# A planner's durations set to the trace, and a tile's scores ordered behind the values of the tile ahead

## The chip, the core and the metric

The kernel runs on one core of a Trainium2 chip. The metric is the device time of one execution in microseconds (us), as the median of several runs. In the profile PE is TensorE (matmuls), PEld its weight loads, DVE is VectorE, ACT is ScalarE, POOL is GpSimd and SP is the engine whose queue issues nearly all transfers.

## What is computed

The input x is 8 sequences of 512 tokens with 256 channels, all in float32. The program is a sandwich of three blocks:

```
x = x + 0.5 * ffn(layernorm(x))      # "local" block, two layers
x = x + attn(layernorm(x))           # global attention, 16 heads of 16 channels
x = x + 0.5 * ffn(layernorm(x))      # the local block again, same weights

ffn, for each of 2 layers:
  h = shift_token(x)                 # second half of the channels one token later
  q, k, v = split(h @ wqkv)          # 8 heads of 64
  q, k = rotary(l2norm(q) * qs), rotary(l2norm(k) * ksc)
  x = x + local_attention(q, k, v) @ wo     # windows of 128: own and previous window
  h = layernorm(shift_token(x)) * lg + lb
  a, g = split(h @ w1 + b1)
  x = x + (a * gelu(g)) @ w2 + b2
attn, for each of 16 heads:
  softmax(y y^T / 4) x, then times a 256x256 slice of the weight, summed over heads
```

## The kernel before

Three streams of work run side by side. Streams 0 and 1 each take eight local blocks, for the even and the odd sequences (`stream`, `attention`, `glu`). The third, `global`, does the global attention of a sequence as soon as its first local block is done (`global_heads`), and fills the holes of the other two. A sequence's 512 tokens are four tiles of 128. In `attention` a tile goes through `front` (projections, norms, rotary), `scores` (matmuls of q and k, mask and maximum, exp, division), `values` (probabilities times v) and `project`. Scores and values come in two groups of four heads, `g` = 0 and 1; each group has one buffer of probabilities, `work_p`, of which a stream has two.

The first and the last local block of a stream turn the probabilities on TensorE. All others are "far" (`far` is true): they are turned by VectorE in 32x32 pieces and by a round trip through DRAM. There `turned_quarters` writes a buffer with two transfers to `dram_quarters` and reads it back with four; `turned_far` does the same for smaller ones with one write. Both run on SP's queue.

Nothing is issued when it is written down. The code records operations in a `Plan`; every call becomes an `Op`, and consecutive matmuls inside `plan.together()` become one. `Plan.order` is then a list scheduler over five engines. It gives each operation a time that the engine is busy and a time until its result is there (`Plan.cost`), knows which operations each one must follow (`op.after`, found from the tiles that they read and write), and picks again and again the operation that can start earliest by its model; among those that can start within 40 ns of it, the one recorded first (`rank`). It also decides which slot of a buffer or PSUM bank a tile gets. `Plan.issue` emits the instructions in that order, so the planner's durations decide the order in which each engine's queue stands, and nothing else. All five engines run their queues in order and wait on semaphores. As every instruction is emitted from `issue`, all carry one line number in the profile, and groups are told apart by tile names.

The planner knows that TensorE's array works in several shapes (`op.mode`: whole, 64x64 "quarters", 32-row "fours") and charges 150 ns (290 into "fours") for a change of shape (`Plan.MODE`); a matmul in another shape than the last one gets a rank 100 lower in priority (`Plan.STICK`). A change of ScalarE's function table is charged 1283 ns (`Plan.TABLE`). Transfers go through one modelled pipe (`pipe`):

```
            if op.calls[0][0] == "dma_start":
                a = op.calls[0][2]["out"]
                pipe = max(pipe, op.start + 2000.0) + elements(a) * a.shape[0] * 4 / 170
                op.end = pipe + 300
```

The number at the end is bytes per ns. The functions that the change touches:

Of the kernel before, what the change touches and what calls it, by code (L numbers as in the profile page):

```python
# [13 lines left out]
PSUM, DRAM = bass.MemoryType.PSUM, bass.MemoryType.DRAM  # L14

P = 128
# [153 lines left out]
def elements(a):  # L170
    n = 1
    for d in a.shape[1:]:
        n *= d
    return n


class Plan:
# [55 lines left out]
    def cost(self, op):  # L233

        if op.engine == "tensor":

            lanes, op.mode = {}, "whole"
            for name, args, kw in op.calls:
                lane, t = 0, 109.0
                if name == "matmul":  # L240
                    a = kw["lhsT"]
                    lane, t = (a.region()[0], args[0].region()[0]), 2 * max(0.842 * elements(kw["rhs"]), 0.852 * a.shape[1])
                    k, m = a.shape
                    op.mode = "fours" if k <= 32 else "quarters" if k <= 64 and m <= 64 else "halves" if k <= 64 else "columns" if m <= 64 else "whole"
                lanes[lane] = lanes.get(lane, 0.0) + t
            busy = max(lanes.values())
            return busy, busy + 170
        name, args, kw = op.calls[0]
        n = max(elements(a) for a in (*args, *kw.values()) if hasattr(a, "shape"))
        if name == "dma_start":  # L250
            return 580.0, 2300.0
        if op.engine == "scalar":
            if name == "activation":
                op.mode = {AF.Exp: "exp", AF.Gelu: "gelu"}.get(args[2])
                busy = 70 + 0.82 * n + (105 if "bias" in kw else 0)
                return (busy + 93, busy + 310) if "accum_out" in kw else (busy, busy + 110)
            return 70 + 0.81 * n, 175 + 0.81 * n
        if op.engine == "vector":
            if name == "tensor_tensor_reduce":
                return 90.0 + n, 250.0 + n  # L260
            if name == "bn_stats":
                return 70.0 + n, 150.0 + n
            return 90 + 1.035 * n, 170 + 1.035 * n
        if name == "memset":
            return 80 + 0.85 * n, 100 + 0.85 * n
        if ALU.pow in args:
            return 350.0 + 157 * n, 400.0 + 157 * n
        return 210 + 1.98 * n, 250 + 1.98 * n

    def order(self):  # L270

        for op in self.ops:
            op.busy, op.done = self.cost(op)
            op.waits = len(op.after)
            for o in op.after:
                o.before.append(op)

            for t in op.tiles:
                if t.users[0] is op:
                    source = [] if t.ring.space == PSUM else [u for u in op.tiles if u.ring.space == PSUM and u.users[0] is not op]  # L280
                    (source[0].users[0] if source else op).opens.append(t)
        for op in self.ops:
            op.opens.sort(key=lambda t: t.turn)
            for t in op.opens:
                for o in t.users:
                    if o is not op:
                        op.admits.append(o)
                        o.waits += 1
        free, mode = dict.fromkeys(self.ENGINES, 0.0), dict.fromkeys(self.ENGINES)
        pipe = 0.0  # L290
        candidates = {e: [op for op in self.ops if op.engine == e and not op.waits] for e in self.ENGINES}
        order = []

        def slots(op):

            need, turns, at = {}, {}, 0.0
            for t in op.opens:
                k, i = need.get(t.ring, 0), turns.get((t.ring, t.stream), 0)
                need[t.ring], turns[t.ring, t.stream] = k + 1, i + 1
                if t.ring.space != PSUM:  # L300

                    k += t.ring.missing(t.stream, t.turn) - i
                if len(t.ring.free) <= k:
                    return None
                at = max(at, t.ring.free[k][0])
            return at

        while len(order) < len(self.ops):
            best = None
            for e in self.ENGINES:  # L310
                when = []
                hold = min((op.rank for op in candidates[e] if len(op.opens) > 4 and op.ready <= free[e]), default=None)
                for op in candidates[e]:
                    if op.opens:
                        at = slots(op)
                        if at is None:
                            continue
                        if hold is not None and op.rank > hold and op.opens[0].ring.space == PSUM:
                            continue
                        at = max(at, op.ready, free[e])  # L320
                    else:
                        at = max(op.ready, free[e])
                    when.append((at, op))
                if when:
                    t = min(at for at, _ in when)
                    if best is None or t < best[0]:
                        best = t, e, when
            assert best is not None, "the plan is stuck"
            t, e, when = best
            change = self.MODE.get(mode[e], 0.0) if e == "tensor" else self.TABLE if e == "scalar" else 0.0  # L330
            switch = lambda op: change if op.mode is not None and op.mode != mode[e] else 0.0
            at, op = min(
                ((at, op) for at, op in when if at <= t + 40), key=lambda c: (c[1].rank + (self.STICK[e] if switch(c[1]) else 0), c[0])
            )
            candidates[e].remove(op)
            op.start = at + switch(op)
            mode[e] = op.mode or mode[e]
            free[e] = op.start + op.busy
            op.end = op.start + op.done
            if op.calls[0][0] == "dma_start":  # L340
                a = op.calls[0][2]["out"]
                pipe = max(pipe, op.start + 2000.0) + elements(a) * a.shape[0] * 4 / 170
                op.end = pipe + 300
            for x in op.opens:
                _, x.slot = x.ring.free.pop(0)
                x.ring.open(x.stream, x.turn)
            for x in op.tiles:
                x.left -= 1
                x.end = max(x.end, op.end)
                if not x.left:  # L350
                    x.ring.free.append((x.end + self.SIGNAL, x.slot))
                    x.ring.free.sort()
            for o in op.before:
                if o.engine != e:
                    o.ready = max(o.ready, op.end + self.SIGNAL)
                elif e != "tensor":
                    o.ready = max(o.ready, op.end)
            for o in op.before + op.admits:
                o.waits -= 1
                if not o.waits:  # L360
                    candidates[o.engine].append(o)
            order.append(op)
        return order
# [12 lines left out]
def macaron(ctx: ExitStack, tc: tile.TileContext, x, weight, wqkv, wo, w1, w2, b2, vecs, qk_scales, rotary, out):  # L376
# [87 lines left out]
    for i, sign in enumerate((1, -1, 1)):  # L464
# [5 lines left out]
            base=0,  # L470
# [95 lines left out]
    def attention(k, y, l, far):  # L566
# [2 lines left out]
        tiled = lambda t, c: y[:, t, c * P : (c + 1) * P]  # L569
        nc.scalar.copy(z0[:, :N], transposed(tiled, 0))  # L570
        z1 = shifted(tiled, k)
        v = {}

        kT = work.tile([P, NPAIR, 2, P], F32, tag=f"kT{k}", bufs=1)

# [54 lines left out]
        def scores(t, pair, rn):  # L630
# [21 lines left out]
            for g in range(2):  # L652
# [16 lines left out]
                with plan.together():  # L669
                    for i in range(2):  # L670
                        keys = kT[:, 2 * g + i].rearrange("p j k -> p (j k)")
                        for q, to, ks in sorted(pieces, key=lambda piece: piece[1].start - piece[1].stop):
                            for par in range(2):
                                rows = slice(par * DH, (par + 1) * DH)
                                nc.tensor.matmul(
                                    sps[par][q, i, to], lhsT=qT[rows, 2 * g + i, q], rhs=keys[rows, ks], start=True, stop=True
                                )
                heads = slice(4 * g, 4 * g + 4)

                if far:  # L680
# [51 lines left out]
        def values(t, probs):  # L732
# [25 lines left out]
            if far:  # L758
                for g in range(2):
                    with plan.together():  # L760
                        for i in range(2):
                            products(
                                2 * g + i,
                                lambda par, own, rows, q: probs[g][rows, own * (nk - 1), q.start // 32 : q.stop // 32, 2 * i + par, :],
                            )
            else:
                turned = []
                for n in range(NPAIR + 2):
# [370 lines left out]
```

## Time and profile before

| | us |
|---|---|
| median of 3 runs | 3949.23 (3947.79 to 3949.27) |
| the profiled execution's own time | 3952.0 |
| its span, first to last instruction | 3950.1 |
| PE busy (matmuls) | 3878.5 |
| VectorE, ScalarE, GpSimd busy | 2447.9, 1766.9, 1233.7 |

The span holds 26240 records of matmuls, since each float32 matmul stands as two, and some are missing. A row of groups reads: line, engine, operation, tile written and tiles read, shape, count; then busy time, mean ns of one, and the engine's idle time just before with what ended it. A row of waits reads: engine and tile that waited, who released it, us in total, times, longest. A row of windows reads: the stretch and its length, busy us and instructions of each engine, then the granted clock of TensorE, the share of the transfer engines and GB/s. Matmuls overlap in their records, so that one's record is longer than the time until the next one starts.

### The profile page before, as it was taken

Reading aid. Unit: us, or ns where it says so; the run is one execution under the profiler, and the core shown is the slowest. Engines: PE = TensorE matmul, PEld = TensorE weight load, DVE = VectorE, ACT = ScalarE, POOL = GpSimd, SP = SyncE. Lnnn points to the kernel's source line nnn. Section 1 sums busy time; section 2 is a strip of 40 time slices with the busy share of each in tenths; the row PEclk is TensorE's granted clock in tenths of the full one; section 3 lists DMA queues with packets and bytes.
Section 4 is the critical chain, followed back from the end, with each engine's and each line's share of the span. In section 5 each row is a group of like instructions: output and inputs, shape, how many; then the busy total and the mean of one; then the engine's idle time right before and its main releaser. Section 6 shows DMA issues by size and latency. Waiting matters only on the chain.

```text
span 3950.1 us, 72878 instructions
## 1 busy us (share of the span) xinstructions
PE 3878.5 (98%) x26240; PEld 2659.5 (67%) x26240; DVE 2447.9 (62%) x6888; ACT 1766.9 (45%) x4548; POOL 1233.7 (31%) x1132
## 2 busy tenths in 40 slices
PE   8999999999999999999999999999999999999998
PEld 4566776766767667677676776767767667686665
DVE  7676655667566665674765747657466565535674
ACT  5565534535344353452443534535335353324564
POOL 6242323424133341341422405324133242103240
PEclk9999999999999999999999999999999999999999
DMA  3000543534435344253442534525335244110000
GB/s 116 1 24 27 155 135 104 150 98 140 129 104 153 93 128 143 88 165 92 128 138 94 155 104 130 159 91 156 91 116 157 81 143 134 61 33 9 1 24 11
DMA packets 437644, 400.74 MB, mean 101 GB/s; under 512 B 53954, under 2 KB 379172, under 8 KB 437284
## 3 DMA queue, kind: packets, MB, share of 16 engines
q1 hardware_dynamic: 436420, 394.76, 33.5%
q8 instruction: 208, 3.41, 0.4%
q10 hardware_dynamic: 864, 1.33, 0.1%
q14 instruction: 152, 1.25, 0.1%
HBM read 235.49 MB, written 143.66 MB: 96 GB/s over the span
## 4 chain that ended last, share of the span: by engine, by line
PE 81%; DVE 5%; issue 2%; ACT 2%; POOL 1%; DMA 0%; SPq 0%; DVEq 0%; POOLq 0%; ACTq 0%
PE psum_bank L369 81%; ACT work_p L369 2%; DVE work_p L369 2%; DVE work_qn L369 1%; DVE small_ss L369 1%; POOL small_rn L369 0%; POOL work_t L369 0%; ACT work_both L369 0%; DVE work_xw L369 0%; DVE small_bnst L369 0%; SPq L369 0%; DVE work_both L369 0%; DVE work_o L369 0%; DVE xpool_x L369 0%; POOL small_rstd L369 0%
## 5 line engine op out<-in xcount | busy, mean ns | idle before, releaser
L369 PE MATMUL psum_bank<-work_xw,work_e 128*128 128x256 f32 x4096 | 960.0, 385 | 3.0 <-ACT work_e L369 1.9
L369 PEld LDWEIGHTS psum_bank<-work_xw,work_e 128*128 128x128 f32 x4096 | 765.8, 191 | 199.0 <-issue 47.2
L369 PE MATMUL psum_bank<-wpool_wqkv,zpool_z 128*128 128x512 f32 x1536 | 712.2, 603 | 2.7 <-ACT work_v L369 2.0
L369 ACT ACTIVATE work_p<-work_p,small_nmax,small_rn 128x192 f32<-128x192 f32 (+2 forms) x1024 | 543.7, 533 | 324.2 <-DVE small_nmax L369 213.7
L369 POOL TENSOR_TENSOR work_t<-work_qn,const_tab 128x256 f32<-128x256 f32 x512 | 397.4, 797 | 590.3 <-ACT work_qn L369 503.5
L369 PE MATMUL psum_bank<-zpool_z,wpool_w 128*128 128x512 f32 x1280 | 558.9, 595 | 1.5 <-DVE zpool_z L369 1.5
L369 POOL TENSOR_TENSOR small_rn<-small_ss,const_nhalf 128x8 f32<-128x8 f32 x256 | 484.4, 1893 | 149.8 <-DVE small_ss L369 141.6
L369 POOL TENSOR_TENSOR work_p<-work_p,small_ri 128x768 f32<-128x768 f32 (+1 forms) x192 | 264.4, 1378 | 778.9 <-DVE small_ri L369 371.9
L369 ACT ACTIVATE work_e<-psum_bank 128x512 f32<-128x512 f32 x512 | 298.3, 596 | 420.4 <-PE psum_bank L369 403.9
L369 PE MATMUL psum_bank<-work_wa,work_gz 128*128 128x256 f32 x2048 | 477.6, 381 | 5.9 <-DVE work_gz L369 3.9
L369 PEld LDWEIGHTS psum_bank<-wpool_wqkv,zpool_z 128*128 128x128 f32 x1536 | 284.8, 192 | 288.1 <-issue 266.4
L369 PEld LDWEIGHTS psum_bank<-zpool_z,wpool_w 128*128 128x128 f32 x1280 | 243.5, 191 | 301.8 <-issue 273.7
L369 PEld LDWEIGHTS psum_bank<-work_wa,work_gz 128*128 128x128 f32 x2048 | 385.3, 190 | 78.3 <-issue 14.7
L369 DVE SCALAR_TENSOR_TENSOR xpool_x<-psum_bank,gsmall_rinv,xpool_x 128x256 f32<-128x256 f32 x512 | 242.2, 474 | 283.6 <-PE psum_bank L369 281.2
L369 ACT COPY work_qn<-psum_bank 128x512 f32<-128x512 f32 x256 | 148.4, 582 | 327.1 <-PE psum_bank L369 263.8
L369 DVE SCALAR_TENSOR_TENSOR work_p<-psum_bank,const_vec,work_p 128x512 f32<-128x512 f32 x128 | 95.7, 749 | 278.1 <-PE psum_bank L369 226.9
L369 PE MATMUL psum_bank<-wpool_wo,work_o 128*128 128x256 f32 x1024 | 244.9, 383 | 6.4 <-DVE work_o L369 6.2
L369 PE MATMUL psum_bank<-wpool_w,work_p 128*128 128x256 f32 x1024 | 243.2, 380 | 0.0
L369 DVE COPY work_xw<-psum_bank 128x512 f32<-128x512 f32 x256 | 173.8, 680 | 108.4 <-PE psum_bank L369 107.9
L369 DVE TENSOR_REDUCE small_ss<-work_sq 128x8 f32<-128x512 f32 x256 | 172.2, 673 | 109.0 <-ACT work_sq L369 108.1
L369 PEld LDWEIGHTS psum_bank<-wpool_wo,work_o 128*128 128x128 f32 x1024 | 191.4, 190 | 56.7 <-DVE work_o L369 16.1
L369 ACT ACTIVATE work_p<-psum_bank,const_vec 128x512 f32<-128x512 f32 x128 | 87.9, 687 | 296.6 <-PE psum_bank L369 288.0
(89 smaller groups left out, 4943.3 us busy)
## 6 DMA issues: line engine op xcount, KB each, us to landing
work_p<-dram_quarters SPq DMA_DIRECT2D x576, 128.0 KB
dram_quarters<-work_p SPq DMA_DIRECT2D x288, 192.0 KB
dram_turned<-work_both SPq DMA_DIRECT2D x96, 512.0 KB
work_both<-dram_turned SPq DMA_DIRECT2D x384, 128.0 KB
work_wa<-in_weight_dram SPq DMA_DIRECT2D x128, 256.0 KB
wpool_w<-in_w_dram SPq DMA_DIRECT2D x48, 640.0 KB
work_hT<-work_gz SPq DMA_DIRECT2D x512, 32.0 KB
dram_turned<-work_p SPq DMA_DIRECT2D x48, 256.0 KB
```

The costliest lines, as they stand in the source:

```text
L369: getattr(getattr(nc, op.engine), name)(*map(real, args), **{k: real(a) for k, a in kw.items()})
```

## The change

It has two parts. The planner's durations are changed in `Plan.cost` and `Plan.order`: transfers, ScalarE, VectorE and GpSimd get the durations that the trace shows; a transfer now occupies its queue for 450 or 560 ns instead of 580, the pipe runs at 330 bytes per ns instead of 170, and a queue that has eight transfers in flight must wait for the first of them (`flying`). And in far blocks each group of scores must be ordered behind the last recorded matmul groups of the values of the tile ahead, both groups (`latest`). Both are on TensorE, so that this constrains the order alone. No operation is added, removed or resized.

```
         if name == "dma_start":
-            return 580.0, 2300.0
+            source = kw["in_"]
+            far = isinstance(source, View) and source.tile.ring.space == DRAM
+            return (560.0 if len(source.shape) > 3 and far else 450.0), 2400.0 if far else 1900.0
         if op.engine == "scalar":
+            base = 60 if args[1].tile.ring.space == PSUM else 100
             if name == "activation":
                 op.mode = {AF.Exp: "exp", AF.Gelu: "gelu"}.get(args[2])
-                busy = 70 + 0.82 * n + (105 if "bias" in kw else 0)
-                return (busy + 93, busy + 310) if "accum_out" in kw else (busy, busy + 110)
-            return 70 + 0.81 * n, 175 + 0.81 * n
+                busy = base + 0.82 * n + (105 if "bias" in kw else 0)
+                return (busy + 92, busy + 280) if "accum_out" in kw else (busy, busy + 105)
+            return base + 0.81 * n, base + 105 + 0.81 * n
         if op.engine == "vector":
             if name == "tensor_tensor_reduce":
-                return 90.0 + n, 250.0 + n
+                return 86.0 + n, 190.0 + n
             if name == "bn_stats":
-                return 70.0 + n, 150.0 + n
-            return 90 + 1.035 * n, 170 + 1.035 * n
+                return 60.0 + n, 145.0 + n
+            pointers = sum(isinstance(u, View) and elements(u) == 1 for u in args[1:])
+            busy = 70 + 1.035 * n + (55 if pointers and name == "scalar_tensor_tensor" else 27 * pointers)
+            return busy, busy + 85
         if name == "memset":
             return 80 + 0.85 * n, 100 + 0.85 * n
         if ALU.pow in args:
-            return 350.0 + 157 * n, 400.0 + 157 * n
-        return 210 + 1.98 * n, 250 + 1.98 * n
+            return 248.0 * n - 10, 248.0 * n + 30
+        busy = 140 + (2.14 if n <= 2 * P else 1.67) * n
+        return busy, busy + 45
...
-        pipe = 0.0
+        pipe, flying = 0.0, []
...
-                pipe = max(pipe, op.start + 2000.0) + elements(a) * a.shape[0] * 4 / 170
-                op.end = pipe + 300
+                pipe = max(pipe, op.start + op.done - 400) + elements(a) * a.shape[0] * 4 / 330
+                op.end = pipe + 400
+                flying = sorted(flying + [op.end])[-8:]
+                if len(flying) == 8:
+                    free[e] = max(free[e], flying[0])
...
-        v = {}
+        v, latest = {}, []
...
+                if far and t > 0:
+                    plan.ops[-1].after.update(latest)
...
+                    latest[g:] = [plan.ops[-1]]
```

The line with `after.update` stands in `scores` behind a group's matmuls, and the one with `latest[g:]` in `values` behind a group's matmuls. In the planner n is the largest number of elements per partition among an operation's operands.

## Prediction

> **What bounds the kernel now.** I began with the page: the share of each engine, then the slices.
>
> ```profile
> span 3950.1 us, 72878 instructions
> PE 3878.5 (98%) x26240; PEld 2659.5 (67%) x26240; DVE 2447.9 (62%) x6888; ACT 1766.9 (45%) x4548; POOL 1233.7 (31%) x1132
> ```
>
> TensorE (PE) is busy 98%; it is idle 3950.1 - 3878.5 = 71.6 us in all. No other engine passes 62%. A shorter program therefore needs either fewer idle microseconds on PE or a cheaper stream of matmuls on it. Next I asked for busy time by stretch, cut where the filler stream (the `global` stream) begins and ends:
>
> ```profile
> core 0: us, PE busy (x) PEld busy (x) DVE busy (x) ACT busy (x) POOL busy (x), PEclk, DMA share, GB/s
> 0.00:330.00 330.00, 299.94 (x2331) 185.35 (x2332) 233.27 (x678) 197.30 (x462) 132.34 (x141) 0.99 0.13 42
> 330.00:3590.00 3260.00, 3244.09 (x21435) 2259.76 (x21437) 1990.10 (x5570) 1370.39 (x3646) 1002.11 (x897) 1.00 0.40 118
> 3590.00:3951.00 361.00, 334.48 (x2479) 214.43 (x2479) 224.57 (x641) 199.24 (x442) 99.26 (x94) 0.97 0.03 10
> ```
>
> In the 3260 us of the middle PE is idle 15.9 us. The other 55.7 us are idle in the head (30.1, of which 15 stand before its second group of matmuls) and the tail (26.5, less the 0.9 by which the last window overhangs). The waits of PE in the middle are single short ones, none by a DMA (the first four rows):
>
> ```profile
> PE psum_bank L369 <- DVE work_gz L369: 3.9, 5, 1.0
> PE psum_bank L369 <- DVE work_o L369: 3.1, 6, 1.1
> PE psum_bank L369 <- ACT work_e L369: 2.7, 3, 1.2
> PE psum_bank L369 <- DVE small_peak L369: 1.7, 2, 1.2
> ```
>
> So an edit of the planner can win little by removing waits. It can win by the order of the matmuls themselves, because PE loses time between matmuls of different array shapes. The timeline shows this as late starts, not as idle time:
>
> ```profile
> 1007.93 2.11 PE L369 MATMUL psum_bank<-work_xw,work_e 128*128 128x256 f32 x9
> 1009.96 0.90 PE L369 MATMUL psum_bank<-work_p,work_v 64*64 64x128 f32 x32
> 1010.79 1.14 PE L369 MATMUL psum_bank<-work_hT 16*128 16x512 f32 x8
> 1011.86 0.48 PE L369 MATMUL psum_bank<-work_xw,work_e 128*128 128x256 f32 x1
> ```
>
> Inside a stretch 128x256 records start 216 ns apart: nine take 1.94 us, but the next shape starts after 2.03, 0.09 late. That late start is only the visible part; the rest sits in the first weight loads after the switch, which nothing hides.
>
> **The change, part by part.** It adds and removes no matmul, copy or DMA: 13696 matmuls and 2618 SP transfers stand in both built programs. New durations change only the order, on every engine, and with it the waits. Three things follow.
>
> **1. Fewer switches of array shape.** I priced a switch by fitting all stretches of the timeline: time from the first matmul of a stretch to the first of the next, less idle gaps, as (records by shape) x (ns of one) plus one constant per kind of switch. It gives 215.8 ns for a 128x256 record, 429.2 for 128x512, 26.7 for a 64-row one of 128, and per switch 197 ns from whole array to 64x64, 186 back, 201 from whole to 16-row, 173 from 64x64 to 16-row; the median residue is 7 ns. The switch out of a 16-row stretch can't be told from the stretch's own time, and costs the same to either shape.
> In the order of instructions before changes shape 850 times, after 686 times: whole to 64x64 315 to 230, back 283 to 204, 64x64 to 16-row 59 to 36, whole to 16-row 67 to 90. All 164 are lost in the middle (696 to 532); head and tail keep 79 and 75. Sum: 85 x 197 + 79 x 186 + 23 x 173 - 23 x 201 ns = 16.7 + 14.7 + 4.0 - 4.6 = 30.8 us less PE time. It lies wholly where PE is the bound, so it should reach the end of the span. Low end: the 0.09 us seen at 1009.96 alone, x 164 = 15 us. High end: 0.20 x 164 = 33 us.
> Why they vanish: scores of a tile's first group used to run ahead of the values of the previous tile's second group, with whole-array work between them. Stretches of values fall from 244 to 188, of scores from 176 to 140. The new dependency is inside PE, so it adds no semaphore.
> The Trainium skill (Trainium Kernel Development and Optimization, Performance Expectations) warns that matmul busy time says little of the distance to the machine's limit, because matmuls are pipelined, and by it the 67% of the weight loads would leave a third to win. The trace shows where part of that lies: the fit puts some 850 x 0.19 = 160 us of switches inside the 98%.
>
> **2. Less room for the round trip through DRAM.** Far tiles send probabilities through DRAM: max-add, exp, Pool's multiply, transpose, two writes, four reads, values. In the trace I could follow 166 of 192 such buffers into their values. From the first max-add to the last landing takes 22.6 us in the median (5% under 15.1, 75% under 26.4), and the values then start 4.7 us after the landing (5%: 1.1; 25%: 3.3). This cover is why no DMA stands among PE's waits. By the order, with the fitted durations, scores and values stood 29.3 us of PE work apart in the median and 20.1 at 5%; now it is 23.8 and 17.3. The new model is the cause: a read of `dram_quarters` lands 2.9 us after its issue by the trace, and the planner's old rate of 170 GB/s in one pipe made four of them later than they are.
> Against that, the trip gets shorter. Of its 22.6 us, 2.3 are a read waiting in SP's queue after its write has landed and 3.7 the second write queued behind others (medians). Between a write and its first read-back stood 5.0 other DMAs on average, now 3.1: at 0.49 to 0.61 us an issue that is about 1 us, and the planner's limit of eight in flight makes the queue's order fit the machine's. The longer DVE, ACT and Pool steps stay (7.7 us to the end of the transpose). A trip without queueing needs about 16 us, under the 17.3 at 5%.
> So some values will wait. If every one comes 2 us earlier than now against its landing, the measured margins give 16 us of raw waits; for 3.5 us, 69; for 5.5 us, 244. A wait of PE gives the same slack to everything else in flight (two streams with two buffers each), so I count a quarter: 4, 17 and 61 us. I take the first, near the row of 1 us saved in the queue and most of the rest in shorter queueing: +4 us. Below nothing: the 15.9 us of middle idle could shrink too, since distances under 2 us from a matmul through DVE or ACT to its dependant get rarer (of `ypool_y` 44 to 15 matmuls, of `work_both` 8 to 0, though of `kT` by DVE 7 to 20); bound -8 us.
>
> **3. ScalarE's tables.** The order has 112 table loads instead of 100. At 1.283 us and 0.30 idle each (128.3 and 30.1 us over 100) that is 12 x 1.58 = 19 us on an engine that is 45% busy: nothing on the path, as long as the exp steps have the slack of part 2. Without that cover at most one load per trip, 12 x 1.3 = 16 us.
>
> ```profile
> L369 ACT ACT_TABLE_LOAD x100 | 128.3, 1283 | 30.1 <-DMA wpool_wqkv<-in_wqkv_dram 14.1 <-PE psum_bank L369 11.6 <-DVE small_nmax L369 3.1
> ```
>
> The skill (ScalarE: Activation LUTs, What ACT_TABLE_LOAD costs) speaks against this change: a switch costs a drain as well, 2.66 us in all. By it ScalarE would pay 32 us, not 19; still inside its idle time.
>
> The other edits cost nothing by themselves. Pool's power over 128x8 is planned at 1974 ns instead of 1606 (row: 1893), Pool's multiply over 768 at 1422 instead of 1731 (row: 1478): the plan follows the rows more closely, and no engine but PE is near its limit. Head and tail keep their PE work (some 308 and 306 us) and their distances, so I leave their idle time as it is.
>
> **Sum.** The profiled execution took 3952.0 us (span 3950.1 and 1.9 around it): 3952.0 - 30.8 + 4 = 3925.2. The median of the runs is 2.8 lower, 3949.2, so 3922.4.
>
> **Rivals.**
> A (0.62), the forecast: switches pay, new waits stay small. 3949 - 33 - 8 = 3908 to 3949 - 15 = 3934.
> B (0.17), the round trip eats it: values come some 3.5 us closer to their landing, 17 us of waits and a few 16 us table loads on the trip: 3934 to 3957. For it: the cover is halved at 25%. Against: the queue is planned better.
> C (0.14), slower: PE waits for the round trip because trips stay 22.6 us long while scores and values move 5.5 us closer. Place: values' matmuls after reads of `dram_quarters`, in the middle. Price 61 - 31 = +30, so about 3980; it decides once such waits pass 31 us, 0.16 us for each of 192 buffers. For it: planned latency (2.8 us for a read) now has no margin over the 2.9 seen. Against: the trip contains 6 us of queueing that the same plan shortens.
> D (0.07): waits of the middle, head and tail shrink as well, 15 us more than A's centre: 3895 to 3908.
> That the change does nothing is excluded by the changed order.
>
> **The numbers.** I predict A's centre, 3922. A measurement can tell about 0.2%, 7.9 us: faster is below 3941.3, slower above 3957.1. Faster: A, D and 0.07 of B (its part below 3941) = 0.76; same 0.10; slower 0.14. The range 3900 to 3955 leaves out C, a part of D and the last of B, 0.18.
>
> **What would show it.** PE busy about 31 us lower in the middle stretch at the same record counts, idle of the middle below 25 us, and still no large row "PE <- DMA" among the waits. Wrong if PE's busy time doesn't fall (the fit's price isn't a price of switches), or if waits at `work_p` reads appear with tens of us.

## The result, and the profile after

The changed kernel takes 4042.7 us (median of 5 runs, 4038.3 to 4044.1), before 3949.2: 1.0236 times as long (95% interval 1.0222 to 1.0251), 93 us slower. I had predicted 3922, faster. The first lines of its page, as they were read before:

```profile
span 4036.9 us, 72678 instructions
PE 3901.8 (97%) x26240; PEld 2697.6 (67%) x26240; DVE 2447.1 (61%) x6888; ACT 1778.7 (44%) x4560; POOL 1229.9 (30%) x1132
```

PE's idle time rose from 71.6 to 135.1 us, and PE's busy time rose by 23 us where I expected 31 less, at the same 26240 records (none is missing, other than I had written: 12544 matmuls stand as two and 1152 transposes as one). The waits of PE show the new item at the top, which did not exist before (columns: us in total, times, longest):

```profile
PE psum_bank L381 <- DMA work_p<-dram_quarters: 33.8, 42, 2.3
PE psum_bank L381 <- DVE ypool_y L381: 17.7, 6, 13.3
PE psum_bank L381 <- ACT work_both L381: 15.3, 15, 2.5
PE psum_bank L381 <- DVE work_p L381: 10.1, 10, 4.3
```

The busy time by stretch, cut at the first and last matmul of the global heads, before and then after:

```profile
363.00:3603.00 3240.00, 3225.21 (x21285) 2248.15 (x21286) 1968.82 (x5514) 1357.92 (x3629) 992.97 (x889) 1.00 0.40 118
3603.00:3951.00 348.00, 321.48 (x2417) 203.60 (x2415) 219.58 (x627) 196.41 (x433) 99.26 (x94) 0.97 0.03 10
```

```profile
366.00:3676.00 3310.00, 3241.62 (x21283) 2277.69 (x21284) 1971.24 (x5512) 1383.20 (x3651) 989.90 (x889) 0.99 0.39 116
3676.00:4037.00 361.00, 328.23 (x2419) 210.01 (x2417) 217.86 (x628) 182.22 (x423) 99.33 (x94) 0.95 0.03 10
```

The middle is 70 us longer and the tail 13; the head moved by 3. In the middle PE is idle 68.4 instead of 14.8 us, and still busy 16 us more. Where that comes from is seen around one wait:

```profile
2197.07 1.88 PE L381 MATMUL psum_bank<-wpool_wqkv,zpool_z 128*128 128x512 f32 x4
2198.88 1.14 PE L381 MATMUL psum_bank<-work_hT 16*128 16x512 f32 x8
2201.49 0.44 PE L381 MATMUL psum_bank<-work_p,work_v 64*64 64x128 f32 x4 [1.48 <-ACT work_e L381]
2202.92 1.55 PE L381 MATMUL psum_bank<-work_p,work_v 64*64 64x128 f32 x28 [0.99 <-DMA work_p<-dram_quarters]
2204.40 3.78 PE L381 MATMUL psum_bank<-wpool_wqkv,zpool_z 128*128 128x512 f32 x4
2208.11 1.51 PE L381 MATMUL psum_bank<-work_p,work_v 64*64 64x128 f32 x32
```

```profile
2199.00:2202.60 3.60, 1.45 (x12) 0.41 (x12) 3.53 (x8) 3.52 (x10) 3.51 (x4) 1.00 0.73 197
2202.60:2209.40 6.80, 6.48 (x64) 3.85 (x68) 1.42 (x3) 0.58 (x1) 2.11 (x1) 0.50 0.59 195
```

The values stand at the head of PE's queue; their probabilities have not landed, so PE waits 1.48 and then 0.99 us. (The first of these rows names an exp of ScalarE, which ended at 2201.43; the second of the four reads landed only at 2201.36.) Just then the granted clock falls to 0.50 (third number from the end) for 6.8 us, and the same four 128x512 records that took 1.88 us at 2197.07 take 3.78 at 2204.40. The wait of 2.5 us costs some 3.4 us more, and those count as busy.

I split both spans with the fit of the prediction: the array's work by record shape, the changes of shape at the fitted prices, idle gaps, half of the time at a clock of 0.5, and a rest, which is waits too short to show because a record is longer than the distance to the next one, and the fit's own error.

| us | before, middle | after, middle | before, tail | after, tail |
|---|---|---|---|---|
| array work | 3099 | 3099 | 289 | 289 |
| changes of shape | 109.0 | 78.2 | 14.2 | 14.2 |
| idle | 14.8 | 68.4 | 19.4 | 26.6 |
| lost to the slow clock | 8.5 | 32.4 | 10.2 | 17.1 |
| rest | 9.9 | 33.7 | 5.6 | 5.0 |

The tail's columns stop at the first matmul of the last stretch, some 9 us before the end.

The 31 us of switches are gone, at the fit's prices; 54 us of idle, 24 of slow clock and 24 of rest took their place in the middle. For the buffers that can be followed (144 after, 166 before) the values start 2.7 us after the last landing in the median instead of 4.7, 0.4 instead of 3.3 at 25%, and at 5% the first matmul of a values stretch stands 1.2 us ahead of it (a stretch can start with matmuls on its other buffer).

### The profile page after: what moved, and what is told of

Its sections match the earlier page's. It is cut to its first block, busy times and chain, and to the rows that moved or that the text cites. A ratio compares the mean times of both kernels' runs of the same rounds, so it can differ in the third digit from the quotient of the medians.

```text
span 4036.9 us, 72678 instructions
## 1 busy us (share of the span) xinstructions
PE 3901.8 (97%) x26240; PEld 2697.6 (67%) x26240; DVE 2447.1 (61%) x6888; ACT 1778.7 (44%) x4560; POOL 1229.9 (30%) x1132
## 4 chain that ended last, share of the span: by engine, by line
PE 66%; DVE 8%; DMA 6%; SPq 4%; ACT 4%; issue 3%; POOL 1%; DVEq 0%; POOLq 0%; ACTq 0%
PE psum_bank L381 66%; SPq L381 4%; DVE work_p L381 3%; ACT work_p L381 3%; DMA work_p<-dram_quarters 2%; DVE work_qn L381 1%; DMA dram_quarters<-work_p 1%; DVE small_ss L381 1%; DMA work_p<-dram_turned 1%; DMA dram_turned<-work_p 1%; POOL small_rn L381 0%; DVE work_both L381 0%; DMA dram_turned<-work_both 0%; DMA work_both<-dram_turned 0%; DVE xpool_x L381 0%
## 5 line engine op out<-in xcount | busy, mean ns | idle before, releaser
L381 DVE STREAM_TRANSPOSE work_p<-work_p 128x768 f32<-128x768 f32 (+2 forms) x216 | 202.3, 937 | 61.4 <-POOL work_p L381 60.3
```

The costliest lines, as they stand in the source:

```text
L381: getattr(getattr(nc, op.engine), name)(*map(real, args), **{k: real(a) for k, a in kw.items()})
```

## The experiments

Theory M: the planner now counts the trip through DRAM shorter than it turns out, values come to PE before their data, and the waits drag the clock down. Rival L: the dependency of scores on values makes the waits. Rival C: the durations of VectorE, ScalarE and Pool do. Rival O: any new order costs or gains tens of us by chance. The planner's own times bear out the first step of M: by them the trip, from the first max-add to the last landing, takes 25.5 us in the median before, where the trace has 22.6, and 18.0 in the changed kernel, where the trace has 19.6. So the plan's error turned from 3 us too long to 1.6 too short. In the table, "switches" counts the changes of array shape in the order of instructions, "cover" is the start of the values less the last landing (5% / median, us), and the last three columns are idle, slow clock and rest of the middle.

| run | us | ratio to before (interval) | switches | cover | idle | clock | rest |
|---|---|---|---|---|---|---|---|
| before | 3949 | | 850 | 1.1 / 4.7 | 15 | 9 | 10 |
| changed | 4043 | 1.0236 (1.0222 to 1.0251) | 686 | -1.2 / 2.7 | 68 | 32 | 34 |
| e1 | 3999 | 1.0131 (1.0113 to 1.0149) | 700 | -0.9 / 2.4 | 56 | 24 | 31 |
| e2 | 3927 | 0.9948 (0.9929 to 0.9966) | 793 | 1.4 / 4.8 | 12 | 5 | 8 |
| e3 | 4048 | 1.0255 (1.0239 to 1.0270) | 694 | -1.3 / 2.9 | 70 | 39 | 34 |
| e4 | 3942 | 0.9986 (0.9977 to 0.9995) | 799 | 2.0 / 5.0 | 9 | 2 | 4 |
| e5 | 3964 | 1.0046 (1.0030 to 1.0062) | 744 | -0.2 / 2.6 | 25 | 3 | 20 |
| e6 | 3965 | 1.0047 (1.0031 to 1.0064) | 793 | 2.5 / 5.1 | 19 | 14 | 12 |
| e7 | 3932 | 0.9962 (0.9949 to 0.9975) | 870 | 2.1 / 4.7 | 8 | 0 | 5 |
| e8 | 3958 | 1.0028 (1.0017 to 1.0039) | 711 | 1.7 / 6.0 | 24 | 12 | 18 |
| e11 | 3953 | 1.0014 (1.0005 to 1.0023) | 799 | 1.8 / 4.8 | 14 | 3 | 8 |
| e12 | 4008 | 1.0158 (1.0143 to 1.0173) | 701 | -1.2 / 2.4 | 56 | 31 | 34 |
| f1 | 3994 | 1.0121 (1.0106 to 1.0136) | 686 | -0.9 / 3.7 | 43 | 29 | 26 |
| f2 | 3946 | 0.9997 (0.9988 to 1.0006) | 850 | 2.1 / 5.7 | 14 | 7 | 11 |
| f3 | 3927 | 0.9952 (0.9936 to 0.9969) | 771 | 1.6 / 4.6 | 8 | 2 | 7 |

**Which part does it: e1 to e4.** e1 is before with the new transfer model alone:

```
-            return 580.0, 2300.0
+            return (560.0 if len(source.shape) > 3 and far else 450.0), 2400.0 if far else 1900.0
...
-                pipe = max(pipe, op.start + 2000.0) + elements(a) * a.shape[0] * 4 / 170
-                op.end = pipe + 300
+                pipe = max(pipe, op.start + op.done - 400) + elements(a) * a.shape[0] * 4 / 330
+                op.end = pipe + 400
+                flying = sorted(flying + [op.end])[-8:]
+                if len(flying) == 8:
+                    free[e] = max(free[e], flying[0])
```

> Only the new transfer model (durations, rate, eight in flight); all else as before. Theory M (the planner now counts the trip through DRAM too short, so that values reach PE before their probabilities land, and each wait also slows TensorE's clock): slower than before by most of the 93 us, 4010 to 4050 us, with some 30 us of PE waits for reads of dram_quarters. Rival L (the new dependency of scores on values makes the waits): no slower than before, 3915 to 3950, as 700 instead of 850 changes of shape save 28 us. Rival C (VectorE, ScalarE and Pool durations do it): 3915 to 3950 too.

It took 3999 us, half of the loss, with waits that before does not have; M's 4010 was missed by 11 us. Its first wait row:

```profile
PE psum_bank L375 <- DMA work_p<-dram_quarters: 22.2, 34, 2.3
```

e2 is before with the dependency alone (the lines with `latest`).

> Only the dependency of scores on the values of the tile ahead; all durations as before. M: faster than before, as 793 instead of 850 changes of shape save 57 x 0.188 = 11 us and the distance of scores to values stays 29.6 us in the median: 3930 to 3945. L: slower, 3990 to 4050. C: 3930 to 3945.

3927 us, faster than both kernels, a little below M's range. L falls. e3 is the changed kernel without those lines:

```
-                if far and t > 0:
-                    plan.ops[-1].after.update(latest)
...
-                    latest[g:] = [plan.ops[-1]]
```

> All the new durations, without the new dependency (694 changes of shape, distance of scores to values 23.9 us). M: as slow as the changed kernel, 4025 to 4060. L: 3915 to 3950. C: 4025 to 4060.

4048: the dependency is innocent from this side too. It has 100 table loads like before, so the 12 more of the changed kernel are no cause either. e4 is the changed kernel with the old transfer model (the first diff backwards).

> The changed kernel with the old transfer model (580 and 2300 ns, 170 bytes per ns, no limit in flight); new compute durations and the dependency stay (799 changes of shape, distance 30.5 us in the median). M: 3930 to 3950, no PE waits for reads of dram_quarters over 5 us in all. L and C: 4010 to 4050.

3942, with 15 us of idle, slow clock and rest in its middle, where before has 35: the new compute durations do no harm there, and C falls as the main cause. Beside the new transfer model they do matter: e1 without them lost 49 us, with 22.2 us of waits for `dram_quarters`, and e3 with them 99, with 35.8.

**How thin the cover is: e5, e6, e11.** e5 and e6 are the changed kernel with a later landing planned for reads of more than three dimensions, which are all the reads of `dram_quarters` and of `dram_turned`:

```
-                op.end = pipe + 400
+                op.end = pipe + 400 + (2000.0 if op.calls[0][2]['in_'].shape and len(op.calls[0][2]['in_'].shape) > 3 else 0.0)
```

> The changed kernel, but the planner counts the landing of reads with more than three dimensions (the reads back from DRAM among them) 2 us later. By order 744 changes of shape and 24.5 us from scores to values in the median. M (thin cover at the landing): about half of the loss given back, 3970 to 4010. Rival O (any new order costs some tens of us by chance, the cover has nothing to do with it): 4020 to 4060, or anywhere without a trend towards the next run.

3964, even less than M's 3970. The row of DMA waits falls to a sixth:

```profile
PE psum_bank L381 <- DMA work_p<-dram_quarters: 5.9, 9, 0.9
```

e6 has 4500.0 there.

> As the run before, 4.5 us later: 793 changes of shape, 26.8 us from scores to values. M: the loss is gone, 3925 to 3955, no PE waits for dram_quarters over 5 us. O: no trend, 3990 to 4060.

One wait for `dram_quarters` is left, of 2.1 us, but the time stays at 3965, a miss of 10 us. Against e5 there are 49 more changes of shape, and 10 us more are lost to the slow clock in the middle; together they cost about what idle and rest gave back, 14 us. So there is a trend up to 2 us and none beyond. In e11 one number of the changed kernel goes back:

```
-                pipe = max(pipe, op.start + op.done - 400) + elements(a) * a.shape[0] * 4 / 330
+                pipe = max(pipe, op.start + op.done - 400) + elements(a) * a.shape[0] * 4 / 170
```

> The changed kernel with one number set back: the modelled pipe runs at 170 instead of 330 bytes per ns. 799 changes of shape and 30.0 us from scores to values. M, with the slow pipe as the cover: 3930 to 3960 and no PE waits for dram_quarters over 5 us. If the cover was in the latencies, the issue times or the limit of eight: 4000 to 4050.

3953, without a wait for `dram_quarters`. The slow modelled pipe was the cover: with it the planned trip is 25.3 us again.

**How much an order costs by chance: e7, e12.** e7 is before, e12 the changed kernel, each with `SIGNAL = 115.0` instead of 110.0.

> The kernel before with one unrelated constant of the planner nudged (110 to 115 ns for a signal): a new order throughout (870 changes of shape, 29.4 us from scores to values), cover unchanged. M: 3945 to 3965, the 20 more changes of shape cost 4 us. O: anywhere between 3930 and 4040, so that a single order's time says little.

3932, 16 us faster than before with 20 more changes of shape: below M's range. O holds to this degree, and the 22 us of e2 are not much more than a nudge gives.

> The changed kernel with the signal constant at 115 instead of 110 ns: another order throughout, with the same thin cover (701 changes of shape, 23.9 us from scores to values). M: 4015 to 4060, the loss belongs to the cover. Rival O (this one order was unlucky): back towards 3930 to 3990.

4008: 35 us less than the changed kernel and 7 below M's range, but still 61 over before, with 36.8 us of waits for `dram_quarters`. So two thirds of the loss stay with the thin cover in another order; a third belongs to this one order.

**The landings themselves: f1, f2.** Both keep the order of their kernel on every engine. When the reads of `dram_quarters` are emitted, after the planning, each is made to fetch a quarter of its data, 32 instead of 128 KB; the rest of the probabilities stays untransposed between the 32-row blocks:

```
+                if name == "dma_start" and isinstance(kw["in_"], View) and kw["in_"].tile.shape[1] == 2 * N + 4:
+                    kw = {k: a[:, :, :1] for k, a in kw.items()}
```

> The changed kernel in its own order on every engine; each of the four reads back from dram_quarters fetches a quarter of its data (the rest of the probabilities is left untransposed between the 32-row blocks), so it is issued and lands earlier. M (values wait for landings, and the waits slow the clock): the trip gets 1.5 to 2.5 us shorter, PE waits for dram_quarters fall from 34 to under 5 us, the clock recovers partly, 3960 to 4000 us. If the order costs its time in another way: 4025 to 4045.

3994, 49 us less than the changed kernel with the same instructions in the same order. A read lands 2.1 us after its issue instead of 2.9, and the trip takes 18.0 instead of 19.6 us. The waits did not vanish, as I had expected, but fell:

```profile
PE psum_bank L383 <- ACT work_both L383: 15.1, 15, 2.5
PE psum_bank L383 <- DMA work_p<-dram_quarters: 13.6, 17, 1.9
```

> The same small reads in the kernel before, in its own order: there the reads have cover. M: no change that matters, 3935 to 3952. If transfers cost the kernel time in another way (contention, SP's queue): 3900 to 3935.

The same cut does nothing to before (0.9997), where the reads have cover. So late landings are shown as a cause of at least half of the loss. The other half f1 leaves open: it still has those 13.6 us of waits, and 43 us of idle and 29 of slow clock in the middle.

**The price of a change of shape: e8 to e10.** e8 is e2 with `STICK` for tensor 300 instead of 100.

> The new dependency alone with old durations, and a matmul in another shape ranked 300 lower instead of 100: 711 changes of shape, 29.6 us from scores to values. M with the price of 0.188 us a change: 82 fewer changes than the dependency alone, 15 us less than its 3927: 3905 to 3920. If fewer changes of shape cost waits by themselves, as in the changed kernel: 3960 and over.

3958: 82 changes of shape fewer than e2 and 31 us slower, with good cover (M had 3905 to 3920). Fewer changes did not pay here, since idle, slow clock and rest of the middle grew by 29 us, against a counted gain of 11 there. e9 and e10 measure the price apart from the planner's choices. Their order is that of before; in `project` of the global heads stands, with `:HALF` in e9 and `:P` in e10,

```
+                        if i:
+                            nc.tensor.matmul(pv[:HALF, 1, :32], lhsT=zT[0][:HALF, :HALF], rhs=w[:HALF, 0, :32], start=True, stop=True)
```

> The kernel before in its own order, with one small 64x64 matmul of 32 columns put between the two halves of each of the 256 projections of the global heads (its result is overwritten); the planner counts it as nothing. It adds 512 changes of shape, whole to 64x64 and back. If a change of shape costs the fitted 0.19 us, this is 98 us slower than the next run, which has the same extra matmul in whole shape; if only the 0.09 us of the late start count, 46 us; if the drain is hidden, under 15 us.

> The control of the run before: the same 256 extra matmuls of 32 columns in the same places and the same order, in whole shape. Each pays a weight load of some 0.19 us and its columns twice, so about 256 x 0.3 = 80 us over before, 3990 to 4040, at 850 changes of shape.

4040.5 and 3998.2: 42.3 us apart for 512 changes, 0.083 us each, not 0.19. The control has costs of its own that make this number too small: its weight loads of 0.19 us are not hidden behind 32 columns, and one extra matmul delays the next by 0.22 us in its timeline. In that of e9 one delays by 0.425 us; less twice the 0.08 us between its two records, 0.13 a change is left. The two timelines alone, 0.425 less 0.22, give 0.10 a change; the runs give less because the profiled e10 lost 19.7 us to the slow clock and e9 11.1. So 0.08 to 0.13 here, where the fit over real stretches says 0.19.

**Two orders that beat both kernels: e2 and f3.** f3 is e2 with `"quarters": 190.0` instead of 150.0.

> The dependency alone on the old durations, with a change of shape to 64x64 planned at 190 instead of 150 ns: 771 changes of shape, 29.5 us from scores to values. M: 22 changes fewer than the dependency alone, its cover kept: 3915 to 3940.

3927.4, like e2. Both are half a percent faster than before; against the 16 us of a mere nudge that is no proof of a mechanism.

## Why the prediction was wrong

**What held.** PE is the bound, and the counts of changes of shape were right. The kernel after fits the same prices (206, 192, 199 and 165 ns for the four kinds, where before gave 197, 186, 201 and 173). SP's queueing got shorter as argued: the trip takes 19.6 instead of 22.6 us. Rival C of the prediction, the wait for the round trip, named the mechanism, its place and its row, at 0.14.

**The step that failed: part 2, +4 us.** The shift that I assumed was about right: I took 2 us less cover and got 2.0 in the median, 2.9 at 25%, 2.3 at 5%. By the same margins that gives 16 to 69 us of raw waits, and 33.8 were measured on reads of `dram_quarters`, the sign that I had named for being wrong. Three things were wrong about their price. I counted a quarter, because a wait gives slack to everything else in flight; the waits came in full, and other waits in the middle grew beside them (idle without that row from 15 to 35 us). I left out the short waits that the records hide: the rest grew by 24 us. And I left out TensorE's clock. In before it had fallen to 0.50 nine times, for 46 us; after, 24 times, for 111. That is 24 us more lost in the middle and 7 in the tail, and it stood in the windows view that I had quoted, as 0.99 and 0.97.

The Trainium skill (TensorE: Matmul & The Clock Gate, Part 1) tells of a gate that halves the clock by windows of about 3.4 us of activity. The spells here last 3.4 us or two or three times that, which agrees. The page lets an idle window throttle; in the trace of after, 21 of the 24 spells follow 3.4 us in which PE was idle only 1.0 to 2.7 us, so part of a window can be enough. Which part can be read from the trace, since all spells begin on one grid of 3.413 us. In the middle of after, all 10 steps of this grid with 1.9 to 2.7 us of idle time were followed by a spell, 4 of the 20 with 1.0 to 1.6, and 1 of 920 with less (steps inside a spell left out). Nor are waits the only way into a spell: the four in the middle of before follow steps with 0 to 0.7 us of idle time. Those steps, and the one without idle time in after, hold 1.6 to 3.2 us of `work_hT` matmuls, which use 16 rows of the array; that the few rows count as little activity is likely, but was not tried.

**Part 1, -30.8 us.** The middle does hold 31 us less of switches by the fit, but the direct measurement bounds the price from below at 0.08, so the saving lies between 14 and 31 us. Its reason was wrong: I gave it to the new dependency, but without it the count is 694, and with it alone 793. The new transfer model did it, the same edit that took the cover: e1 alone has 700. How a shorter planned trip brings fewer changes was not tried. Over the runs few changes and much waiting go together (e8 with cover, e1, e3, e12 without), so a saving counted from the order should not have been taken as free.

**Part 3, nothing.** The row after:

```profile
L381 ACT ACT_TABLE_LOAD x112 | 143.7, 1283 | 89.1 <-PE psum_bank L381 45.8 <-DVE small_nmax L381 24.5 <-issue 17.1
```

12 loads more, 15.4 us busy, and ScalarE idle longer before them; e3 has 100 loads and takes as long, and e12 has 138 and is 35 us faster, so they stayed off the path. Of the drain that I had counted in as a possible cost the trace shows nothing: in the median a load begins 0.02 us after the instruction ahead of it, and the next one 0.01 us after the load's end.

**The tail** I left as it was, and it cost 13 us. All kernels with the new compute durations and the old signal constant have 26.6 to 27.6 us idle there, those without 19 to 25 (e1 and e2 19.4); e12 has 21.4. Which duration does it was not tried.

## What to carry to other kernels

When a planner's or scheduler's latency is corrected towards the measured one, first look at how far ahead of need the data arrive in the trace of before: an estimate that is too long may be the cover of everything that is too short. Then price a wait on TensorE at more than its length, since waits of 2 us here halved the clock for the next 3.4 us or more, and don't discount it for the slack it gives to others. And before a few tens of us are explained by a mechanism, nudge an unrelated constant: here that alone moved the time by 16 and 35 us.

## What the runs showed of the hardware

Granted clock: it fell to 0.50 for 3.4 to 10.2 us at a time, always at a step of a grid of 3.413 us, after 1.9 us of idle time or more in the step in all 10 cases in the middle of after, and after 1.0 to 1.6 us in 4 of 20. At 0.50 four 128x512 records took 3.78 instead of 1.88 us. A single 64x64 matmul of 32 columns between whole-array ones cost 0.365 us of the run's time (93.4 us over 256), a whole-shape one 0.20.
